# Attention values by Strassen's seven products for the eight longest pairs of query tiles

## The chip, the cores and the metric

The kernel runs on one core of one Trainium2 chip. A core has a matrix engine (PE, with its weight loads shown apart as PEld), a vector engine (DVE), a scalar engine (ACT), a general engine (POOL), and a queue that here only issues transfers (SP). Each engine works through its own list of instructions in order; engines wait for each other by semaphores. The metric is the device time of one execution in microseconds (us), as the median of several runs.

## The reference

A layer norm of x (2 sequences of 2048 tokens, 512 wide) feeds a causal attention and, beside it, a mixture of eight experts; the result is x + attention * silu(experts). Everything is FP32. Cut to what the change touches:

```python
scores = jnp.einsum('bsk,btk->bst', q, k) * scale
scores = jnp.where(causal[None], scores, -jnp.inf)
attn = jax.nn.softmax(scores, axis=-1)
out = attn @ v
...
x = x + s * g
```

## The kernel before

The program has three stages. The first normalises x, projects queries (with the key projection folded in) and values (with the output projection folded in), and routes tokens to experts. The second runs the experts. The third, from about 632 us on, is the attention; the change is in it alone.

The order of all instructions is written out by hand (`tc.manual_schedule()`): each engine's list is what the Python code emits for it, in that order. Tiles come from pools with a fixed number of buffers; a tile that needs a buffer still in use makes its first writer wait.

**Attention by steps.** A query tile is 128 rows; there are 16 tiles per sequence, 32 in all, taken in the order of `seq`. A key block is 512 keys (`kp2`, `vp` hold such blocks of keys and values). A query tile whose causal range is n times 128 keys is said here to have length n. The main loop (the last `for s` of the kernel) does in step s:

1. `fetch_inputs` of a tile, which loads its rows of x; `attended(s-3)`: ACT scales the finished values out of PSUM (L978), DVE adds the normed x (L981); `emit(s-4)`: POOL multiplies by the gate and adds x (L989, L990), and SP stores.
2. `chunk_scores(s, j)`: for each key block, four matmuls into one PSUM bank of pool `ps_a` (L836), then DVE masks (L841) and takes the row maximum (L842). Between these, `join_p(s-1, j)`: DVE puts the two 16-bit halves of the transposed probabilities of step s-1 together again (L922).
3. `divisor(s-1)`, then `end_scores(s)`: the maximum over the blocks (L854).
4. `exponentials(s)`: ACT takes exp of each block (L907), POOL splits it into two 16-bit halves (L911), SP issues a transposing transfer for each (L916).
5. `fetch_parts`: SP issues loads of coming key, value and query blocks. In odd steps also `gather_y` (POOL gathers expert outputs, L957) and `gate` (DVE, L968 and L969, two tiles at once; ACT, Silu, L973).
6. `values(s-2)`: n matmuls of 512 columns into one PSUM bank of pool `ps_b` (L933).

So the matrix engine's list is scores(s), values(s-2), scores(s+1), values(s-1), and so on; between the scores of a tile and its values lie the values of step s-2, the scores of s+1, the values of s-1 and the scores of s+2. The last two tiles (`AHEAD`) have their gate made early (`make_ahead`), so that after the last matmul only two DVE operations and a store are left (`emit_ahead`, L1010 and L1011).

The first sequence is taken from its longest tile to its shortest (lengths 16, 15, ..., 1). The second goes, in lengths, 9, 10, 1, 2, 11, 12, 3, 4, 5, 6, 7, 8, 13, 14, 15, 16.

Of the kernel before, what the change touches and what calls it, by code (L numbers as in the profile page):

```python
# [10 lines left out]
F32 = mybir.dt.float32  # L11
BF16 = mybir.dt.bfloat16
I32 = mybir.dt.int32
U16 = mybir.dt.uint16
# [12 lines left out]
def gated_attention_moe(  # L27
# [650 lines left out]

    assert B == 2 and NBB == 4
    seq = [t for t in reversed(range(NBB * BT))]  # L680
    seq += [NBB * BT + t for t in (8, 9, 0, 1, 10, 11, 2, 3, 4, 5, 6, 7, 12, 13, 14, 15)]
    assert all(seq[s] // 2 == seq[s + 1] // 2 for s in range(0, NT, 2))
    fetch_k = fetch(aks, lambda: kp2, kt_d, "k2", "kT")
    fetch_v = fetch(avs, lambda: vp, v_d, "v2", "v")
    NQ = 4
    early = [(fetch_k, b, c) for b in range(NBB) for c in range(ND)]
    early += [(fetch_q, n, c) for n in range(NQ) for c in range(2)]

# [171 lines left out]
    stage_a.close()  # L860
    kp2 = right(att, name="kp2", bufs=NBB)
    qp2 = right(att, name="qp2", bufs=NQ)
    ps_b = psum(att, name="ps_b", bufs=2)
    ps_a = psum(att, name="ps_a", bufs=6)
    sm = right(att, name="sm2", bufs=4)


# [23 lines left out]
    wp.close()  # L891

    left = lambda **k: att.enter_context(tc.tile_pool(reuse_waits="tile", **k))
    pp = left(name="pp", bufs=4)
    php = left(name="php", bufs=4)
    tp = left(name="tp", bufs=2 * NBB)
    vp = left(name="vp2", bufs=NBB + 1)
    op = left(name="op", bufs=4)

    def exponentials(s):  # L900

        _, nm, chunks = scored.pop(s)
        rs = sm.tile([P, NBB], F32, name=f"rs_{s}", tag="rs")
        sums[s], halves[s], turned[s] = rs, [], []
        for j, w in enumerate(widths[s]):
            pr = pp.tile([P, TB], F32, name=f"pr_{s}_{j}", tag="pr")
            nc.scalar.activation(  # L907
                pr[:, :w], chunks[j][:, :w], AF.Exp, bias=nm, accum_out=rs[:, j : j + 1]
            )
            pu = php.tile([P, 2 * TB], U16, name=f"pu_{s}_{j}", tag="pu")  # L910
            nc.gpsimd.tensor_copy(  # L911
                pu[:, : 2 * w].rearrange("p (h d) -> p h d", h=2),
                pr[:, :w].bitcast(U16).rearrange("p (d h) -> p h d", h=2),
            )
            puT = php.tile([P, 2 * BT, P], U16, name=f"puT_{s}_{j}", tag="puT", bufs=6)
            nc.sync.dma_start_transpose(out=puT[:, : 2 * w // P, :], in_=pu[:, : 2 * w])  # L916
            halves[s].append(puT)

    def join_p(s, j):
        w = widths[s][j]  # L920
        pT = tp.tile([P, TB], F32, name=f"pT_{s}_{j}", tag="pT")
        nc.vector.tensor_copy(  # L922
            pT[:, :w].bitcast(U16).rearrange("p (i t h) -> p i t h", t=P, h=2),
            halves[s][j][:, : 2 * w // P, :].rearrange("p (h i) t -> p i t h", h=2),
        )
        turned[s].append(pT)

    def values(s):
        first = place(s)[2]
        po = ps_b.tile([P, D], F32, name=f"po_{s}", tag="b")  # L930
        pairs = [(j, i) for j, w in enumerate(widths[s]) for i in range(w // P)]
        for k, (j, i) in enumerate(pairs):
            nc.tensor.matmul(  # L933
                po, lhsT=turned[s][j][:, ts(i, P)], rhs=avs[first + j][:, i, :],
                start=(k == 0), stop=(k == len(pairs) - 1),
            )
        outs[s] = po

    def divisor(s):
        ri = sm.tile([P, 1], F32, name=f"ri_{s}", tag="ri")  # L940
# [3 lines left out]

    def fetch_inputs(s):
        n = seq[s]
        xt = op.tile([P, D], F32, name=f"xo_{s}", tag="xo", bufs=6)
        nc.sync.dma_start(out=xt, in_=xb[:, n, :])
        gates[s] = [xt]

# [11 lines left out]

    def gate(s):

        g = op.tile([P, 2, D], F32, name=f"g_{s}", tag="g", bufs=4)
        for i in range(2):
            w = [share[k][:, 0, seq[s + i] : seq[s + i] + 1] for k in range(2)]
            nc.vector.tensor_scalar(g[:, i, :], rows.pop((s + i, 0)), w[0], None, ALU.mult)  # L968
# [4 lines left out]
        nc.scalar.activation(g, g, AF.Silu)  # L973

    def attended(s):
        o = op.tile([P, D], F32, name=f"o_{s}", tag="o", bufs=3)
        n = seq[s]
        nc.scalar.activation(  # L978
            o, outs[s], AF.Identity, scale=sums[s], bias=xshift[:, n : n + 1]
        )  # L980
        nc.vector.scalar_tensor_tensor(  # L981
            o, gates[s][0], xscale[:, n : n + 1], o, ALU.mult, ALU.add
        )
        outs[s] = o
# [12 lines left out]
    def make_ahead(s):  # L997
        xt, g = gates[s]
        n = seq[s]
        w = op.tile([P, D], F32, name=f"w_{s}", tag="w", bufs=2)  # L1000
        nc.vector.tensor_scalar(w, g, xscale[:, n : n + 1], 1.0, ALU.mult, ALU.add)
        nc.vector.tensor_tensor(xt, xt, w, ALU.mult)
        nc.vector.scalar_tensor_tensor(
            xt, g, xshift[:, n : n + 1], xt, ALU.mult, ALU.add
        )

    def emit_ahead(s):
        xt, g = gates.pop(s)
        o = op.tile([P, D], F32, name=f"o_{s}", tag="o", bufs=3)
        nc.vector.scalar_tensor_tensor(o, outs.pop(s), sums[s], g, ALU.mult, ALU.mult)  # L1010
        nc.vector.tensor_tensor(o, o, xt, ALU.add)  # L1011
        nc.sync.dma_start(out=ob[:, seq[s], :], in_=o)

    K = NBB
    parts_b = [(0, fetch_v, 0), (1, fetch_v, 1), (1, fetch_v, 2), (2, fetch_v, 3),
               (3, fetch_v, K + 2), (4, fetch_k, K + 2), (7, fetch_v, K + 1), (8, fetch_k, K + 1),
               (11, fetch_v, K), (12, fetch_k, K), (15, fetch_v, K + 3), (16, fetch_k, K + 3)]
    parts_b = [(s, f, b, c) for s, f, b in parts_b for c in range(ND)]  # L1020
    parts_b += [(2 * n - 5, fetch_q, n, c) for n in range(NQ, NT // 2) for c in range(2)]
    parts_b.sort(key=lambda part: part[0])

    def fetch_parts(s, most):
        while parts_b and most and parts_b[0][0] <= s:
# [2 lines left out]
            most -= 1  # L1028

    for s in range(NT + OUT + 2):  # L1030
        if s < NT and s:
            begin_scores(s)
        if s < 3:
            fetch_parts(s, 2 * ND)
        for k in range(NT):
            if s == (NT - 5 if k in AHEAD else k + 1):
                fetch_inputs(k)
        if 0 <= s - 3 < NT:
            (emit_ahead if s - 3 in AHEAD else attended)(s - 3)
        if 0 <= s - OUT < NT and s - OUT not in AHEAD:  # L1040
            emit(s - OUT)
        late = s - 1 if 0 <= s - 1 < NT else None
        joins = list(range(len(widths[late]))) if late is not None else []
        if s < NT:
            for j in range(len(widths[s])):
                if s:
# [2 lines left out]
                    join_p(late, joins.pop(0))  # L1049
        for j in joins:  # L1050
            join_p(late, j)
        if 0 <= s - 1 < NT:
            divisor(s - 1)
        if s < NT:
# [3 lines left out]
            fetch_parts(s, 4)  # L1058

        for k in range(0, NT, 2):  # L1060
            if s == (k - 1 if k in AHEAD else k + 3):
                gate(k)
        for k in range(0, NT, 2):
            if s == (k - 3 if k in AHEAD else k + 1):
                gather_y(k)
                gather_y(k + 1)
        for k in AHEAD:
            if s == min(k, NT - 2):
                make_ahead(k)
        if 0 <= s - 2 < NT:  # L1070
            values(s - 2)
    att.close()

# [43 lines left out]
```

## Time and profile before

| What | Value |
| --- | --- |
| median of 3 runs | 1095.23 us (1094.83 to 1099.15) |
| the profiled execution, time | 1094.91 us |
| the profiled execution, span of its trace | 1093.2 us |
| granted PE clock, mean | 0.999 of full speed |
| PE busy | 1079.4 us, 99% of the span |
| DVE, ACT, POOL busy | 484.5, 323.5, 392.8 us |
| attention scores, PE (L836) | 239.1 us, 640 records |
| attention values, PE (L933) | 238.5 us, 544 records |
| PE idle before L933 | 2.1 us |

An FP32 matmul leaves two records of its weight load and two of its multiplication, so 544 records are 272 matmuls. The number after "x" in a row counts records. "Busy" of a group is the time that at least one of its instructions ran; since matmuls overlap, it is less than the count times the mean duration. "Idle before" is time in which that engine stood still just before these instructions, with what ended it.

### The profile page before, as it was taken

How to read it: one execution, taken by the hardware profiler on the slowest of the kernel's cores; microseconds unless marked ns; L12 is line 12 of the kernel's file. 1: busy time of each engine (PE TensorE's matmuls, PEld its weight loads, DVE VectorE, ACT ScalarE, POOL GpSimd, SP SyncE). 2: the span in 40 equal slices, each digit the busy share in tenths (PEclk: the TensorE clock that was granted, in tenths of full speed). 3: DMA queues.
4: the chain of work that ended last, by engine and by line, in shares of the span. 5: the costliest groups of instructions: out<-in, count | busy, mean ns of one | idle time of the engine just before them, and what ended most of it. 6: DMA issues, size and time to landing. Idle time of an engine off the chain costs nothing.

```text
span 1093.2 us, 10842 instructions
## 1 busy us (share of the span) xinstructions
PE 1079.4 (99%) x3044; PEld 521.2 (48%) x3044; DVE 484.5 (44%) x982; ACT 323.5 (30%) x680; POOL 392.8 (36%) x443
## 2 busy tenths in 40 slices
PE   8999999999999999999999999999999999999998
PEld 3444444444555555555545444444454444444443
DVE  4535441686333333333345342333445565464542
ACT  3232323211333232323256121321323333333220
POOL 2411120002443333333331031443546677575530
PEclk9999999999999999999999999999999999999999
DMA  8989889925999999999985185454567886474520
GB/s 306 245 250 289 251 225 339 299 106 143 185 252 229 224 232 226 230 221 233 219 190 148 34 231 127 128 129 123 157 185 195 254 243 166 142 209 113 128 49 29
DMA packets 306218, 210.03 MB, mean 192 GB/s; under 512 B 238056, under 2 KB 250344, under 8 KB 305136
## 3 DMA queue, kind: packets, MB, share of 16 engines
q1 hardware_dynamic: 284080, 146.91, 54.3%
q0 software_dynamic: 10560, 35.17, 12.4%
q10 hardware_dynamic: 11520, 27.27, 6.7%
q8 instruction: 26, 0.43, 0.2%
q14 instruction: 32, 0.26, 0.1%
HBM read 92.89 MB, written 60.03 MB: 140 GB/s over the span
## 4 chain that ended last, share of the span: by engine, by line
PE 74%; issue 12%; POOL 7%; DMA 3%; ACT 2%; DVE 1%; SPq 1%; ACTq 0%; POOLq 0%; DVEq 0%
PE ph L752 15%; PE py L791 15%; PE ps L836 11%; PE po L933 10%; PE pj L324 10%; PE pj L329 9%; PE pw L200 3%; POOL pu L911 2%; POOL yg L957 2%; DMA puT<-pu 2%; POOL o L990 1%; POOL o L989 1%; PE pg L290 1%; ACT w1c L733 1%; POOL xs L638 1%
## 5 line engine op out<-in xcount | busy, mean ns | idle before, releaser
L933 PE MATMUL po<-v,pT 128*128 128x512 f32 x544 | 238.5, 592 | 2.1 <-DVE ri L941 1.7
L836 PE MATMUL ps<-k,q 128*128 128x512 f32 (+3 forms) x640 | 239.1, 529 | 0.0
L791 PE MATMUL py<-w,ht 128*128 (+3 forms) x408 | 187.1, 593 | 0.0
L836 PEld LDWEIGHTS ps<-k,q 128*128 128x128 f32 x640 | 117.7, 190 | 126.7 <-issue 118.3
L752 PE MATMUL ph<-w,xT 128*128 (+1 forms) x544 | 173.1, 460 | 0.7 <-POOL keep L874 0.7
L933 PEld LDWEIGHTS po<-v,pT 128*128 128x128 f32 x544 | 102.7, 190 | 123.9 <-issue 119.8
L911 POOL COPY pu<-pr 128x1024 uint16<-128x1024 uint16 (+3 forms) x80 | 79.7, 1028 | 209.4 <-ACT pr L907 196.9
L777 ACT ACTIVATE ht<-ht,b1sel 128x128 f32<-128x128 f32 (+3 forms) x237 | 73.1, 375 | 230.7 <-DVE ht L771 230.7
L752 PEld LDWEIGHTS ph<-w,xT 128*128 128x128 f32 (+1 forms) x544 | 97.4, 181 | 73.2 <-issue 34.3
L762 POOL COPY hu<-h 128x704 uint16<-128x704 uint16 x68 | 52.6, 773 | 206.7 <-ACT h L760 155.0
L799 DVE COPY y<-py 128x512 f32<-128x512 f32 x68 | 46.9, 690 | 172.7 <-PE py L791 169.0
L324 PE MATMUL pj<-kT,wqk 128*128 128x512 f32 x256 | 113.2, 595 | 0.0
L329 PE MATMUL pj<-wvo,kT 128*128 128x512 f32 x256 | 113.0, 594 | 0.0
L791 PEld LDWEIGHTS py<-w,ht 128*128 128x128 f32 (+3 forms) x408 | 73.5, 182 | 75.5 <-issue 38.1
L638 POOL DMA_INDIRECT xs<-zu_d,toki x68 | 68.9, 1014 | 69.3 <-DVE toki L538 57.9
L907 ACT ACTIVATE pr<-ps,nm 128x512 f32<-128x512 f32 (+3 forms) x80 | 49.0, 620 | 139.1 <-DVE nm L854 138.9
L981 DVE SCALAR_TENSOR_TENSOR o<-xo,xscale,o 128x512 f32<-128x512 f32 x30 | 28.6, 953 | 133.3 <-ACT o L978 118.6
L334 ACT COPY j<-pj 128x512 f32<-128x512 f32 x64 | 37.4, 584 | 142.8 <-PE pj L329 65.6
L842 DVE TENSOR_REDUCE mx<-ps 128x1 f32<-128x512 f32 (+3 forms) x80 | 48.8, 610 | 65.4 <-PE ps L836 64.3
L247 POOL COPY zu<-z 128x1024 uint16<-128x1024 uint16 x32 | 36.1, 1128 | 115.1 <-DVE z L232 115.1
L324 PEld LDWEIGHTS pj<-kT,wqk 128*128 128x128 f32 x256 | 47.6, 190 | 59.2 <-issue 55.0
L329 PEld LDWEIGHTS pj<-wvo,kT 128*128 128x128 f32 x256 | 47.7, 190 | 58.0 <-issue 55.5
(160 smaller groups left out, 896.6 us busy)
## 6 DMA issues: line engine op xcount, KB each, us to landing
y_d<-y SPq DMA_DIRECT2D x68, 256.0 KB
zu_d<-zu SPq DMA_DIRECT2D x32, 264.0 KB
x<-in_x_dram SPq DMA_DIRECT2D x32, 256.0 KB
kt_d<-kT ACTq DMA_DIRECT2D x8, 1024.0 KB
qt_d<-j ACTq DMA_DIRECT2D x32, 256.0 KB
v_d<-j ACTq DMA_DIRECT2D x32, 256.0 KB
k<-kt_d SPq DMA_DIRECT2D x32, 256.0 KB
q<-qt_d SPq DMA_DIRECT2D x32, 256.0 KB
```

Source lines behind the costliest of these rows:

```text
L324: nc.tensor.matmul(po, lhsT=wqk[:, c, ts(r, P)], rhs=kT[:, c, :], start=(c == 0), stop=(c == ND - 1),)
L329: nc.tensor.matmul(po, lhsT=kT[:, c, ts(r, P)], rhs=wvo[:, c, :], start=(c == 0), stop=(c == ND - 1),)
L638: nc.gpsimd.indirect_dma_start(out=xs, out_offset=None, in_=zu_d, in_offset=bass.IndirectOffsetOnAxis(ap=toki[:, i : i + 1], axis=0),)
L752: nc.tensor.matmul(ph[at, :], lhsT=xT[:, c, at], rhs=rhs[k], start=(c == 0), stop=(c == ND - 1),)
L762: nc.gpsimd.tensor_copy(hu[:, :, :H], h.bitcast(U16).rearrange("p (d h) -> p h d", h=2))
L777: nc.scalar.activation(ht[:hn, c, at], ht[:hn, c, at], AF.Silu, bias=b1sel[:hn, c, j : j + 1])
L791: nc.tensor.matmul(py[at, :], lhsT=ht[:k, c, at], rhs=rhs[n], start=(c == 0), stop=(c == NH - 1),)
L836: nc.tensor.matmul(ps[:, :w], lhsT=aqs[seq[s] // 2][:, c, ts(t % 2, P)], rhs=aks[first + j][:, c, :w], start=(c == 0), stop=(c == ND - 1),)
L842: nc.vector.tensor_reduce(scored[s][0][:, j : j + 1], ps[:, :w], AX.X, ALU.max)
L907: nc.scalar.activation(pr[:, :w], chunks[j][:, :w], AF.Exp, bias=nm, accum_out=rs[:, j : j + 1])
L911: nc.gpsimd.tensor_copy(pu[:, : 2 * w].rearrange("p (h d) -> p h d", h=2), pr[:, :w].bitcast(U16).rearrange("p (d h) -> p h d", h=2),)
L933: nc.tensor.matmul(po, lhsT=turned[s][j][:, ts(i, P)], rhs=avs[first + j][:, i, :], start=(k == 0), stop=(k == len(pairs) - 1),)
```

## The change

Two query tiles and two blocks of 128 keys form a 2x2 block product, as do the two halves of the 512 value columns: A (probabilities, two tiles by two key tiles) times B (two key tiles by two column halves). Done plainly that is eight products of 256 columns (the kernel before does them as four of 512). The change does it with seven, by Strassen's scheme in Winograd's form, for the pairs listed in `FAST`: the four longest pairs of the first sequence and the four longest of the second. A pair of lengths (n1, n2) has m = min(n1, n2) // 2 such blocks; with lengths (15,16), (13,14), (11,12) and (9,10), m is 7, 6, 5 and 4, so 22 per sequence and 44 in all. Key tiles beyond 2m (three per pair) are multiplied plainly, in halves of 256 columns (`product`).

What is added around the products:

- `combine_v(b)`: four DVE operations on each value block; for sequence 1 in steps 1 and 2, between the joins and `end_scores`; for sequence 2 in steps 21, 22, 23 and 25.
- `combine_p(s)`: four DVE operations on m times 128 columns each. In the even step after a pair's scores, all joins and `combine_p` are put ahead of that step's score maxima.
- `values_first` and `values_begin` (even step), `values_end` (odd step) in place of `values`: seven chains of m matmuls, two chains to a PSUM bank (left and right half), with two ACT copies and eight DVE additions of 256 columns between them.
- For the pair of the last two steps but two, `values_begin` is moved one step later; the last pair's gate (`gate`, `make_ahead`) is made in step 32 and not before step 31.

What is moved or resized: the second sequence goes in lengths 7, 8, 1, 2, 5, 6, 3, 4, 9, 10, ..., 16; `parts_b` loads value blocks 0 and 1 before the first transposes and 2 and 3 in step 1; buffers are cut (`pp` 4 to 3, `pu` 4 to 3, `puT` 6 to 5, gathered rows 4 to 2, gates 4 to 2, `xo` 6 to 5, `ps_a` 6 to 5, queries 4 to 3, values 5 to 4 blocks), `ps_b` has 3 banks in place of 2, and `attended` and `emit` of a fast pair come at its fourth and fifth step.

```diff
-    seq += [NBB * BT + t for t in (8, 9, 0, 1, 10, 11, 2, 3, 4, 5, 6, 7, 12, 13, 14, 15)]
+    seq += [NBB * BT + t for t in (6, 7, 0, 1, 4, 5, 2, 3, 8, 9, 10, 11, 12, 13, 14, 15)]
-    ps_b = psum(att, name="ps_b", bufs=2)
-    ps_a = psum(att, name="ps_a", bufs=6)
+    ps_b = psum(att, name="ps_b", bufs=3)
+    ps_a = psum(att, name="ps_a", bufs=5)
...
+    FAST = (0, 1, 2, 3, 12, 13, 14, 15)
...
+    def combine_v(b):
+        n = 1 if b % NBB == NBB - 1 else 2
+        v = avs[b].rearrange("p (i h) d -> p i h d", h=2)[:, :n]
...
+        nc.vector.tensor_tensor(t1, b12, b11, ALU.subtract)
+        nc.vector.tensor_tensor(t2, b22, t1, ALU.subtract)
+        nc.vector.tensor_tensor(t3, b22, b12, ALU.subtract)
+        nc.vector.tensor_tensor(t4, b21, t2, ALU.subtract)
...
+    def combine_p(s):
+        m = min(place_keys(s), place_keys(s + 1)) // 2
...
+        nc.vector.tensor_tensor(s1, a21, a22, ALU.add)
+        nc.vector.tensor_tensor(a21, a11, a21, ALU.subtract)
+        nc.vector.tensor_tensor(s2, s1, a11, ALU.subtract)
+        nc.vector.tensor_tensor(s4, a12, s2, ALU.subtract)
...
+    def chain(dst, a, v, stop=True):
+        n = a.shape[1]
+        for k in range(n):
+            nc.tensor.matmul(
+                dst, lhsT=a[:, k], rhs=v(k), start=(k == 0), stop=(stop and k == n - 1)
+            )
...
+    def values_first(s):
+        p16, u2 = bank(s, "p16"), half_d(s, "u2")
+        chain(p16[:, LO], combos[s][1], raw(s, 0, LO))
+        nc.scalar.copy(u2, p16[:, LO])
+        seven[s] = p16, u2
+
+    def values_begin(s):
...
+        chain(p75[:, LO], s3, vt(s, 2))
+        chain(p16[:, HI], s2, vt(s, 1))
+        nc.scalar.copy(o1[:, LO], u2)
+        add(u2, p16[:, HI], u2)
+        add(u3, p75[:, LO], u2)
...
+    def values_end(s):
...
+        chain(p75[:, HI], s1, vt(s, 0))
+        add(o2[:, HI], p75[:, HI], u3)
+        add(u2, p75[:, HI], u2)
+        p24 = bank(s, "p24")
+        chain(p24[:, LO], a12, raw(s, 1, LO), stop=False)
+        product(p24[:, LO], s, 2 * m, k1, LO, start=False)
+        add(o1[:, LO], p24[:, LO], o1[:, LO])
+        chain(p24[:, HI], a22, vt(s, 3), stop=False)
+        product(p24[:, HI], s + 1, 2 * m, k2, LO, start=False)
+        add(o2[:, LO], p24[:, HI], u3)
+        p03 = bank(s, "p03")
+        product(p03[:, LO], s + 1, 2 * m, k2, HI)
+        add(o2[:, HI], p03[:, LO], o2[:, HI])
+        if s + 1 in AHEAD:
+            emit_ahead(s + 1, o2, slice(0, D))
+            emit_ahead(s, o1, LO)
+        chain(p03[:, HI], s4, raw(s, 1, HI), stop=False)
+        product(p03[:, HI], s, 2 * m, k1, HI, start=False)
+        add(o1[:, HI], p03[:, HI], u2)
...
-    parts_b = [(0, fetch_v, 0), (1, fetch_v, 1), (1, fetch_v, 2), (2, fetch_v, 3),
-               (3, fetch_v, K + 2), (4, fetch_k, K + 2), (7, fetch_v, K + 1), (8, fetch_k, K + 1),
-               (11, fetch_v, K), (12, fetch_k, K), (15, fetch_v, K + 3), (16, fetch_k, K + 3)]
+    parts_b = [(0, fetch_v, 0), (0, fetch_v, 1), (1, fetch_v, 2), (1, fetch_v, 3),
+               (4, fetch_k, K), (6, fetch_v, K), (8, fetch_k, K + 1), (10, fetch_v, K + 1),
+               (12, fetch_k, K + 2), (14, fetch_v, K + 2), (16, fetch_k, K + 3), (18, fetch_v, K + 3)]
...
+    combine = {1: [0, 1], 2: [2, 3], 21: [K], 22: [K + 1], 23: [K + 2], 25: [K + 3]}
...
+        fast = s // 2 - 1 in FAST
...
+        if fast and s % 2 == 0:
+            for j in joins:
+                join_p(late, j)
+            joins = []
+            combine_p(s - 2)
...
+        for b in combine.get(s, []):
+            combine_v(b)
...
-            if s == (k - 1 if k in AHEAD else k + 3):
+            if s == (k + 2 if k in AHEAD else k + 3):
                 gate(k)
...
+        if s == NT:
             for k in AHEAD:
                 make_ahead(k)
-        if 0 <= s - 2 < NT:
+        if fast:
+            if s == NT - 1:
+                values_begin(s - 3)
+            if s % 2:
+                values_end(s - 3)
+            else:
+                values_first(s - 2)
+                if s != NT - 2:
+                    values_begin(s - 2)
+        elif 0 <= s - 2 < NT:
             values(s - 2)
```

## The prediction

> **What bounds the kernel now.** First the page's busy times, then the PE rows with each tile shape apart.
>
> ```profile
> PE 1079.4 (99%) x3044; PEld 521.2 (48%) x3044; DVE 484.5 (44%) x982; ACT 323.5 (30%) x680; POOL 392.8 (36%) x443
> ```
>
> ```profile
> L933 PE MATMUL po<-v,pT 128*128 128x512 f32 x544 | 238.5, 592 | 2.1 <-DVE ri L941 1.7 <-DVE pT L922 0.3
> L836 PE MATMUL ps<-k,q 128*128 128x512 f32 x448 | 196.7, 593 | 0.0
> L836 PE MATMUL ps<-k,q 128*128 128x256 f32 x64 | 15.1, 379 | 0.0
> ```
>
> PE is never waiting: the values stand still for 2.1 us in all, the scores for none. So PE work removed is time gained, but every wait put before PE is time lost, one for one. 593 less 379 says that 256 columns cost about 214 ns per record in a stream; weight loads of one stream start every 0.43 us at 512 columns. So a 512-column FP32 matmul (two records) takes 0.86 us, a 256-column one 0.43 us, with no extra price for the narrower form (its busy time over its count, 236 ns, still holds the ends of 8 short runs and is the upper bound).
>
> Next the timeline around the last scores (step 31), for what DVE, ACT and POOL take. Columns: start us, duration us, engine, line, [idle before].
>
> ```profile
> 1050.02 0.30 DVE L841 TENSOR_TENSOR ps<-ps,keep 128x128 f32<-128x128 f32 x1 [2.14 <-PE ps L836]
> 1051.69 0.14 DVE L854 TENSOR_REDUCE nm<-mx 128x1 f32<-128x4 f32 x1
> 1054.22 1.41 DVE L969 SCALAR_TENSOR_TENSOR g<-yg,share,g 128x512 f32<-128x512 f32 x1
> 1062.04 0.78 ACT L978 ACTIVATE o<-po,xshift,ri 128x512 f32<-128x512 f32 x1 [4.96 <-PE po L933]
> 1062.90 0.75 DVE L981 SCALAR_TENSOR_TENSOR o<-xo,xscale,o 128x512 f32<-128x512 f32 x1 [7.27 <-ACT o L978]
> 1063.57 4.63 DVE L922 COPY pT<-puT 128x1024 uint16<-128x1024 uint16 x4
> 1063.73 1.65 POOL L989 TENSOR_TENSOR o<-o,g 128x512 f32<-128x512 f32 x1 [3.66 <-DVE o L981]
> 1075.75 0.69 DVE L1011 TENSOR_TENSOR o<-o,xo 128x512 f32<-128x512 f32 x1
> ```
>
> The row maximum (nm) is there 1.8 us after the scores end (1049.98), the gate 3.8 us after nm. Four joins take 4.63 us beside POOL's emits; alone they take 0.61 each. A DVE tensor-tensor is 0.29 at 128 columns and 0.69 at 512: estimate 0.43 at 256, 0.69 at 512, 1.09 at 896. Last the one real PE wait, to see what a hand-over costs: the join ended at 848.83, and PE started 0.15 later.
>
> ```profile
> 848.02 0.82 DVE L922 COPY pT<-puT 128x768 uint16<-128x768 uint16 x1 [1.58 <-DMA puT<-pu]
> 848.98 0.67 PE L933 MATMUL po<-v,pT 128*128 128x512 f32 x1 [1.74 <-DVE ri L941]
> ```
>
> [...] The change puts two chains in one bank, and its program does wait there; no run yet shows the price. [...]
>
> **The change part by part.**
>
> *PE work removed.* Per block, four 512-column matmuls (8 x 0.429 = 3.43 us) become seven of 256 (14 x 0.215 = 3.01): 0.41. Times 44: **-18.0** (-9 if a record costs 236 ns against 438.5 for 238.5/544). The 24 leftover key tiles cost the same in halves.
>
> *Added DVE and ACT work* costs nothing as work (DVE is 44% busy): four operations per value block, four per pair of up to 1.09 us, eight adds of 0.43, two small ACT copies. It costs where it stands in line ahead of what PE waits for. I followed the order of each engine's list in the changed program, with the durations above.
>
> *B, bank hand-over.* In `values_end` the right half of p24 waits for the DVE add that reads the left half, and likewise p03. Nothing else is in PE's list between. Price: PE drain 0.16 (379 less 216), DVE start 0.04, add 0.43, restart 0.15, and the second record after a restart comes 0.08 late: 0.85. For p03, six pairs (the last two are under Tail): **+5.1**.
>
> *A, the same for p24, with DVE busy.* In DVE's order the adds stand behind nm and `gate` of that odd step. The add is done at scores' end + 1.3 to 1.9 (nm, read from the timeline in steps 3, 5, 7, 9, 21, 29) + 3.8 (gate) + 0.7 (two adds) + 0.43 + 0.15 = 6.4 to 6.9 us. PE gets there after two chains and one or two leftover tiles, 0.43 each: 6.9, 6.0, 5.2, 4.3 us (m = 7, 6, 5, 4, first sequence), 3.9 and 4.8 (m = 4, 5, second). Stalls 0.85, 1.0, 1.6, 2.5, 3.1, 1.7: **+10.7**.
>
> *C, the s2 chain.* It goes into the bank whose left half ACT copies (u2), and that copy is behind the exponentials of the same step. Scores' end to last exp is 5.6, 4.8, 4.9, 4.5, 4.7 us in steps 4, 6, 8, 20, 28 of before; with 0.55 for copy and restart, less what joins no longer delay, and 1 us more in step 8 where `combine_p` comes ahead of the maxima. PE has two chains, 2m x 0.43 = 5.2, 4.3, 3.5, 3.5, 4.3. Stalls **+6.7** (0.4, 1.0, 2.5, 1.5, 0.9, restarts 0.4).
>
> *Start.* Before: joins of step 0 end 646.9, nm(1) 647.3, scores(2) end 657.4, last join of step 1 659.8, nm(2) 660.1. Now block 1's loads are ahead of the transposes on SP (+1, some of it hidden), then `combine_v` of blocks 0 and 1 (8 x 0.69 = 5.5) precedes nm(1): 653.8. With five score banks, the second block of scores(2) waits for the first exp of tile 1: 654.6 for 648.8, so scores(2) end at 663.2. Joins of step 1 end 12.6 after nm(1) as before: 666.4. `combine_p` 4.4: 670.8. Maxima 2.5: 673.3. `combine_v` of 2 and 3, 4.5: 677.8; nm(2) 678.2; exps 2.6; u2 and restart 0.6: 681.4; s2 chain of 3.0: 684.4. Without stalls the three chains would end at 657.4 + 9.1 = 666.5. **+18**.
>
> *Tail.* Step 31: u3 is behind the gate, s1's chain waits for it, 1.5; A and B for the last two pairs, 4 x 0.85 = 3.4. Step 32: T is the end of `values_end(28)`. DVE first finishes two tiles (add, ACT 0.78, L981 twice: T + 3.0), and only then joins tile 31 and combines. POOL's four emit operations fall on this: joins 2.5 alone, 4.6 beside two, about 6 beside four; then two combinations: s3 at T + 10.4, while PE has one chain (3.0). Stall 7.5. Then s2 and s4, gate 2.5, Silu 1.1, `make_ahead` 3.6, u2, u3 are ahead of s1's chain: 11.2 us, while PE has two chains (6.0): 5.2. **+17.6**. After the last matmul three half-width operations and a half store take the place of two and a store: nothing.
>
> *Middle.* Where tiles are short, the time from the scores' end to the first join is 11 to 12 us (steps 13, 16, 17 of before, where PE did stall). The cover before values(16), (17), (20), (21) is 12, 11, 12, 14 lengths x 0.86 = 10.3, 9.4, 10.3, 12.0, and step 21 has a `combine_v` (2.7) ahead of nm. POOL's smaller buffers and SP's moved loads fall here: the new key and value blocks are issued behind that step's transposes, 1.9 us each, and need free blocks that PE has left a step before. +6 less the stalls of before: **+4** (0 to 10).
>
> Sum: -18 + 5.1 + 10.7 + 6.7 + 18 + 17.6 + 4 = +44. The profiled span 1093.2 becomes 1137; the execution's time is 1.7 above its span and the median 0.3 above that: **1139 us**.
>
> **The rivals.** (1) Only the bank hand-overs cost (A and B at 0.85, 16 times = 13.6), as start and tail find cover: 18 - 13.6 gives 1091, the same; with half of C, A and Tail, 1101 to 1118. For it: ACT and DVE are under half busy. Against: the waits are of order, not of load. (2) **The other side:** the seven products show. The place is `values_end`; if a hand-over costs 0.3 in place of 0.85 and DVE's queue has drained by then, 18 less about 8 gives 1085. It decides where all waits together fall below 18; Start or Tail alone reach that, so it is unlikely. (3) The short tiles become the bound: POOL needs about 6.7 us per step there (4 gathers per two steps, two emits, a copy) against 6.6 of PE, so a backlog delays copies, transposes and values: 20 more, 1152 to 1170. (4) 256-column matmuls are not half: the gain is 9, 1148; it lies within the range. For it only the 236 ns.
>
> **Numbers.** A measurement tells 0.5% (5.5 us) from no change. All waits as listed 0.70 (1119 to 1151, (4) in it); partly covered 0.09; short tiles bound 0.10; same 0.06; faster 0.05. Slower is 0.89. The range 1108 to 1156 takes in the first case, half of the second and half of the third. Its ends also follow from the terms' own: start 10 to 21, tail 12 to 21, middle 0 to 10, gain 9 to 18.
>
> **What would show it.** Right: 256-column records 0.215 us apart in the values; PE idle of some 60 us before the values' lines, put down to the DVE adds, ACT's u2 copy and the combinations; about 18 of it between 645 and 685 and as much in the last 60; gaps of 0.8 us or more in each `values_end`. Wrong: a start without a PE gap (then the V combinations were faster, or nm(1) was not behind them); `values_end` without gaps; or PE idle mostly in the short tiles.

## The result and the profile after

The change makes the kernel slower: 1169.99 us median of 4 runs (1167.6 to 1170.79) against 1095.03 (1094.27 to 1099.15) for the kernel before, a ratio of 1.0673 (95% interval 1.0641 to 1.0704). That is 75 us more, where +44 was predicted; it lies above the range. The profiled span grew by 72.7 us, from 1093.2 to 1165.9.

The page of the changed kernel, busy times first, then the granted PE clock in 40 slices of the span:

```profile
PE 1089.1 (93%) x3356; PEld 588.3 (50%) x3356; DVE 552.4 (47%) x1112; ACT 328.9 (28%) x696; POOL 392.9 (34%) x443
...
PEclk9999999999999999999999889999999999899989
```

PE has less to do and yet is busy for longer (1089.1 for 1079.4): some of its records ran at half pace, which the 8s of the clock line show (the mean granted clock is 0.977, before 0.999). Waits are read from one execution of each kernel; its time stands beside the median in the table of the experiments, since the two are up to 6 us apart. The rows of PE from 630 us on, tile shapes apart (busy, mean ns, idle before and its releasers):

```profile
L836 PE MATMUL ps<-k,q 128*128 128x512 f32 x416 | 185.8, 600 | 7.4 <-ACT pr L908 7.4
L942 PE MATMUL po<-v,pT 128*128 128x512 f32 x144 | 68.0, 619 | 10.5 <-DVE pT L924 8.8 <-DVE ri L1055 1.7
L989 PE MATMUL p<-vT,pT 128*128 128x256 f32 x176 | 49.2, 433 | 25.9 <-DVE pT L981 13.9 <-DVE o L1006 9.9 <-DVE vT L964 2.1
L989 PE MATMUL p<-vT,s 128*128 128x256 f32 x176 | 44.6, 405 | 13.5 <-ACT u L1011 9.0 <-DVE u L1006 4.5
L989 PE MATMUL p<-v,s 128*128 128x256 f32 x88 | 21.1, 388 | 4.1 <-DVE o L1006 4.1
```

Before, these columns held 2.1 us of idle in all; now 65.4 (with the 4.0 us of shorter scores). The releasers are the ones named in the prediction: L981 is the combination that the s3 chain needs, L1006 the adds that free a bank (A and B), L1011 the copy of u2 (C), L908 the exponentials that free a bank of scores. The chains of a pair follow each other on PE as a11, s3, s2 (`values_begin`) and s1, a12, a22, s4 (`values_end`), named by the operand made of probabilities; A is the wait before a22, B that before s4, C that before s2. The L942 row, ordinary values of short tiles, now waits 10.5 us, 8.8 of it for joins. In PE's timeline (start, duration, what, idle before and releaser):

```profile
656.38 11.69 PE L836 MATMUL ps<-k,q 128*128 128x512 f32 x24 [7.41 <-ACT pr L908]
...
679.58 4.75 PE L989 MATMUL p<-vT,s 128*128 128x256 f32 x14 [2.36 <-ACT u L1011]
...
702.95 3.29 PE L989 MATMUL p<-vT,pT 128*128 128x256 f32 x14 [0.52 <-DVE o L1006]
...
989.56 3.60 PE L989 MATMUL p<-vT,pT 128*128 128x256 f32 x8 [5.16 <-DVE pT L981]
996.84 3.55 PE L989 MATMUL p<-vT,s 128*128 128x256 f32 x8 [3.69 <-ACT u L1011]
...
1017.38 3.52 PE L989 MATMUL p<-vT,pT 128*128 128x256 f32 x8 [2.81 <-DVE o L1006]
...
1134.24 6.10 PE L989 MATMUL p<-vT,pT 128*128 128x256 f32 x14 [8.76 <-DVE pT L981]
```

Start, hand-overs, copy of u2 and tail are all there. Two things are not in the prediction: the wait at 989 with most of that at 997, and the durations behind long waits. 14 records of 256 columns take 3.29 us at 702.95 and 6.10 at 1134.24. The 24 records at 656.38 (16 of 512 columns and 8 of 256, merged in one line) take 11.69, where the same 24 take 8.86 in runs shown below: here the ones of 512 columns stand 0.854 us apart for a while, and 0.429 after it.

By stages, from the records of the trace: idle is the gap to the end of the record before, and drain the 0.1 to 0.2 us that this last record takes beyond its usual distance to a next one; slow is the distance between records above 0.429 us x columns/512 where there was no gap.

| Stage (us of the span) | Predicted | Idle and drain | Slow records | Before, both |
| --- | --- | --- | --- | --- |
| 630 to 685, start | 18.0 | 12.7 | 4.0 | 0.0 |
| 685 to 830, first long pairs | 13.7 | 10.8 | 3.0 | 0.2 |
| 830 to 985, short tiles | 4.0 | 15.4 | 5.4 | 2.8 |
| 985 to 1085, second long pairs | 8.9 | 16.3 | 5.4 | 0.1 |
| from 1085, tail | 17.6 | 16.6 | 3.9 | 0.0 |

The columns of after sum to 71.8 and 21.7; less before's 3.1 and less 18 of work that is 72.4, and the spans grew by 72.7. So about 29 us are missing in the prediction: 14 in the short tiles, 13 in the second long pairs, 3 in the tail, less 1 too much at the start. In the short tiles 5.8 us belong to one place: at 966 the third block of scores(25) waits 4.04 us for a bank that the exponentials of step 24 free, and DVE's combinations of V in steps 22 and 23 (5.1 and 2.5 us) stand ahead of nm in that line.

### The profile page after: what moved, and what is told of

Read it like the earlier page. It is cut to its first block, busy times and chain, and to the rows that moved or that the text cites. A ratio compares the mean times of both kernels' runs of the same rounds, so it can differ in the third digit from the quotient of the medians.

```text
span 1165.9 us, 11696 instructions
## 1 busy us (share of the span) xinstructions
PE 1089.1 (93%) x3356; PEld 588.3 (50%) x3356; DVE 552.4 (47%) x1112; ACT 328.9 (28%) x696; POOL 392.9 (34%) x443
## 5 line engine op out<-in xcount | busy, mean ns | idle before, releaser
L836 PE MATMUL ps<-k,q 128*128 128x512 f32 (+3 forms) x640 | 243.9, 537 | 11.5 <-ACT pr L908 11.5
L836 PEld LDWEIGHTS ps<-k,q 128*128 128x128 f32 x640 | 119.6, 194 | 135.5 <-issue 112.0
L908 ACT ACTIVATE pr<-ps,nm 128x512 f32<-128x512 f32 (+3 forms) x80 | 49.1, 621 | 180.8 <-DVE nm L854 180.6
L942 PE MATMUL po<-v,pT 128*128 128x512 f32 x144 | 68.0, 619 | 10.5 <-DVE pT L924 8.8
L989 PE MATMUL p<-vT,pT 128*128 128x256 f32 x176 | 49.2, 433 | 25.9 <-DVE pT L981 13.9
L924 DVE COPY pT<-puT 128x1024 uint16<-128x1024 uint16 (+3 forms) x80 | 58.5, 749 | 31.1 <-DMA puT<-pu 31.1
```

The lines of the kernel that those rows point to most:

```text
L836: nc.tensor.matmul(ps[:, :w], lhsT=aqs[seq[s] // 2][:, c, ts(t % 2, P)], rhs=aks[first + j][:, c, :w], start=(c == 0), stop=(c == ND - 1),)
L908: nc.scalar.activation(pr[:, :w], chunks[j][:, :w], AF.Exp, bias=nm, accum_out=rs[:, j : j + 1])
L924: nc.vector.tensor_copy(turned[s][:, j * TB : j * TB + w].bitcast(U16).rearrange("p (i t h) -> p i t h", t=P, h=2), halves[s][j][:, : 2 * ...
L942: nc.tensor.matmul(dst, lhsT=turned[s][:, ts(k, P)], rhs=avs[first + k // BT][:, k % BT, cols], start=(start and k == k0), stop=(k == k1 - 1),
L989: nc.tensor.matmul(dst, lhsT=a[:, k], rhs=v(k), start=(k == 0), stop=(stop and k == n - 1))
```

## The experiments

The theory at the outset: the waits of the scheme as predicted, and PE's half pace behind them, for the rest. The rivals: the short tiles in their new order are the bound by themselves; the half pace has another cause than idleness; the waits only move when one is removed.

| Run | Median us | Profiled run, us | Ratio to before (95%) |
| --- | --- | --- | --- |
| the change | 1169.99 | 1167.60 | 1.0673 (1.0641 to 1.0704) |
| frame: no products | 1110.64 | 1115.04 | 1.0133 (1.0117 to 1.0150) |
| trim: six pairs | 1139.77 | 1145.45 | 1.0403 (1.0386 to 1.0420) |
| warm: stalls filled | 1172.98 | 1173.72 | 1.0704 (1.0679 to 1.0730) |
| banks: halves in turns | 1156.44 | 1155.68 | 1.0559 (1.0534 to 1.0583) |
| frame_order | 1102.37 | 1100.15 | 1.0052 (1.0034 to 1.0071) |
| frame_banks | 1106.90 | 1104.86 | 1.0102 (1.0073 to 1.0130) |
| u2early | 1161.24 | 1156.74 | 1.0598 (1.0567 to 1.0628) |
| gate_late | 1180.15 | 1179.36 | 1.0771 (1.0749 to 1.0794) |
| best1: six pairs, old order | 1125.61 | 1125.33 | 1.0269 (1.0242 to 1.0296) |
| best2: four pairs, old order | 1090.70 | 1092.19 | 0.9948 (0.9933 to 0.9964) |
| best3: five pairs, old order | 1089.41 | 1088.12 | 0.9944 (0.9927 to 0.9961) |
| plain2: best2 without products | 1099.04 | 1095.92 | 1.0026 (1.0018 to 1.0033) |

### Without the products: what the frame costs

```diff
-    FAST = (0, 1, 2, 3, 12, 13, 14, 15)
+    FAST = ()
```

(`combine_v` is left out; `gate`, `make_ahead` and `emit_ahead` of the last pair go back to their old steps and form, and with them the buffers of `xo` and of the gates to 6 and 4.)

> Every pair gets its values by the ordinary product; the second batch's order, the smaller buffers, the 5+3 PSUM banks and the loads' times are those of the changed kernel. If the loss is the waits of the scheme and the slow clock behind them, the frame alone costs 4 to 8 us over the kernel before: 1099 to 1103. If the short tiles together, the order or the missing buffers bound the middle (rival 3), its 20.7 us of idle and slow records stay although no combination is computed: 1112 to 1120.

Measured 1110.64: 15 us over the kernel before, not 4 to 8, and just under the rival's numbers. PE's timeline of this run:

```profile
651.03 11.91 PE L836 MATMUL ps<-k,q 128*128 128x512 f32 x24 [2.83 <-ACT pr L908]
...
855.87 5.46 PE L942 MATMUL po<-v,pT 128*128 128x512 f32 x6 [3.06 <-DVE ri L1055]
...
880.18 6.25 PE L942 MATMUL po<-v,pT 128*128 128x512 f32 x14 [2.10 <-DVE pT L924]
...
916.16 6.23 PE L942 MATMUL po<-v,pT 128*128 128x512 f32 x10 [3.54 <-DVE pT L924]
```

and its busy times from 830 to 985 (length of the window, then PE, PEld, DVE, ACT, POOL with their counts, clock, DMA share, GB/s):

```profile
830.00:985.00 155.00, 143.82 (x371) 69.13 (x370) 84.91 (x167) 56.66 (x96) 101.58 (x91) 0.97 0.73 204
```

The short tiles lose 17.4 us (12.0 idle and drain, 5.4 slow) with no combination in the program; with the products they lose 20.8. The two sums are not made of the same waits: the frame, which combines no V, has none before scores, so the 5.8 us at 966 are the products' own. And the frame's profiled run is its slowest, 1115.04 us at a mean granted clock of 0.991; the other three took 1109.79 to 1111.11 at 0.995 to 0.997, so some 4 us of slow records and waits are not in the usual run. After 985 the frame has no gap at all, so the 21.7 us there do belong to the products. POOL is busy 101.6 of 155 us: it is not full, so a lack of its throughput is not what holds PE. In each of the six stretches of 15 us from 850 to 940 it was busy for 9.9 to 12.1. What PE waits for is one tile's way from its scores to its last join, 13 to 20 us in steps 14 to 22 (from the ends of the L836 and L924 records).

### Order and banks apart

```diff
-    seq += [NBB * BT + t for t in (6, 7, 0, 1, 4, 5, 2, 3, 8, 9, 10, 11, 12, 13, 14, 15)]
+    seq += [NBB * BT + t for t in (8, 9, 0, 1, 10, 11, 2, 3, 4, 5, 6, 7, 12, 13, 14, 15)]
```

on the frame for frame_order (its loads of keys and values in the order that this wants), and for frame_banks, on the frame too:

```diff
-    ps_b = psum(att, name="ps_b", bufs=3)
-    ps_a = psum(att, name="ps_a", bufs=5)
+    ps_b = psum(att, name="ps_b", bufs=2)
+    ps_a = psum(att, name="ps_a", bufs=6)
```

> The frame run (ordinary products, 5+3 banks, the changed kernel's small buffers) with the second batch in the old order (8, 9, 0, 1, 10, 11, 2 to 7, 12 to 15) and the loads of its keys and values in the order in which that wants them. If the new order is what opens the 17 us of idle and slow records between 830 and 985, they go to 2 or 3 and the time to 1095 to 1099. If the five banks of scores or the smaller buffers open them, the time stays at 1108 to 1112.

> The frame run with 6 PSUM banks for scores and 2 for values, as in the kernel before; the new order stays. If the order is the cause: 1106 to 1111, only the 2.8 us wait at the start goes. If the sixth bank is: 1095 to 1099.

By the ratios the frame's 1.3% falls to 0.5% with the old order and to 1.0% with the sixth bank: the order is worth some 9 us. The bank's 3 us are not set apart from none (the two intervals overlap), but in the trace of frame_banks the wait at the start is gone with its slow records. In frame_order the stage from 830 to 985 has 5.9 us of idle and slow records left. In the old order long tiles stand between the short ones, so the same 13 to 18 us from scores to joins (steps 14 to 19 of that run) lie behind more PE work. The order is the main cause in the middle, though not to the whole extent expected (1095 to 1099; before itself stood at 1098.3 in that session).

PE's timeline of frame_order, for the start and for the wait that answers to the frame's at 855.87:

```profile
650.67 8.86 PE L836 MATMUL ps<-k,q 128*128 128x512 f32 x24 [2.18 <-ACT pr L908]
...
852.47 4.22 PE L942 MATMUL po<-v,pT 128*128 128x512 f32 x6 [3.07 <-DVE ri L1055]
```

The two kernels have the same PE list up to there. The wait at the start differs by 0.65 us (2.83 and 2.18), the 24 records behind it by 3.05 (11.91 and 8.86), and PE comes to the later wait at 852.81 and 849.40, 3.4 us apart. So what half pace costs at the start was still there 200 us on. This part of the difference between the two spans is no merit of the order.

### The ends

```diff
-    FAST = (0, 1, 2, 3, 12, 13, 14, 15)
+    FAST = (1, 2, 3, 12, 13, 14)
-    combine = {1: [0, 1], 2: [2, 3], 21: [K], 22: [K + 1], 23: [K + 2], 25: [K + 3]}
+    combine = {2: [0, 1], 3: [2], 21: [K], 22: [K + 1], 23: [K + 2]}
```

(The last pair goes out in its old form, and `values_begin` is always in the even step.)

> The first and the last pair go back to the ordinary product, six pairs keep the seven products; V is combined in steps 2 and 3. If start and tail cost what the trace of the changed kernel shows (16.7 us of idle and slow records before 685, about 17 of the 20.5 after 1085), and the two pairs give back 14/44 of the 18 us saved (5.7): 1170 - 15 - 17 + 5.7 = 1144 (1139 to 1150). If the stall of the start only moves to the next pair, and that of the tail to the pair before: 1160 or more.

Measured 1139.77, in the theory's range. Two pairs fewer give back 5.7 us of removed work and still the time falls by 30: start and tail together cost about 36 us of the change by the medians, 32 by the waits and slow records of the two traces. How much of that V's combinations ahead of nm(1) and nm(2) cost is not told apart. What is left at the ends is 3.1 us before 685 and 2.2 after 1085.

### A, B and C

For banks, the adds' order follows the chains':

```diff
-        p24 = bank(s, "p24")
+        p24, p03 = bank(s, "p24"), bank(s, "p03")
         chain(p24[:, LO], a12, raw(s, 1, LO), stop=False)
...
+        product(p03[:, LO], s + 1, 2 * m, k2, HI)
+        add(o2[:, HI], p03[:, LO], o2[:, HI])
         chain(p24[:, HI], a22, vt(s, 3), stop=False)
```

For u2early, ahead of `chunk_scores` in the main loop, and no more behind it:

```diff
+        if fast and s % 2 == 0:
+            values_first(s - 2)
```

For gate_late, the loop that calls `gate` is moved behind `values_end` (the last pair's gate stays ahead of `make_ahead`).

> The halves of p24 and p03 take turns (p24 low, p03 low, p24 high, p03 high), so no chain follows at once in the bank of the chain before. If the hand-over waits A and B are what the prediction said, some 16.6 us of gaps go (A 9.8, B 4.1, four of the tail 2.7) and a little of the slow clock: 1152 to 1157. If A's part behind the maxima and the gate only moves one chain on, B's share goes alone: 1164 to 1167.

> The changed kernel with the a11 chain and ScalarE's copy of u2 issued before the scores of the even step (and so before its exponentials) instead of after them. If C is the queue of exponentials ahead of the copy, its gaps before the s2 chains go (2.4 at the start, 0.7, 1.5, 3.7, 0.8 = 9 us, and part of the slow clock), against an a11 chain that may now wait for its joins at the start: 1158 to 1164. If the copy only moves the wait to the u3 sum or the exponentials behind it: 1167 to 1173.

> The changed kernel, with the gate of each pair but the last emitted behind the value sums of its step instead of ahead of them, and nothing else. If the prediction's A is the sum of a bank hand-over (0.68 us) and of the gate and maxima queued ahead on VectorE, the six A gaps (0.68, 0.82, 1.45, 2.33, 2.98, 1.58 us) fall to 0.68 each, 5.8 us together, and the wait for u3 in step 31 (3.42) loses 1 to 2: 1161 to 1164. If the maxima of the scores, not the gate, are what the sums stand behind, the gaps keep most of their length: 1168 or more.

banks came to 1156.44 and u2early to 1161.24, both in the theory's range, though neither gained all that the theory listed. The PE rows of banks that held A and B:

```profile
L989 PE MATMUL p<-vT,pT 128*128 128x256 f32 x176 | 48.5, 430 | 21.2 <-DVE pT L981 13.7 <-DVE o L1006 5.3 <-DVE vT L964 2.2
...
L989 PE MATMUL p<-v,s 128*128 128x256 f32 x88 | 20.3, 379 | 0.0
```

B is gone (4.1 to 0.0), A is down from 9.9 to 5.3: what remains is DVE coming late from maxima and gate, no longer the hand-over. And of u2early, where C stood, with what came new:

```profile
L989 PE MATMUL p<-vT,s 128*128 128x256 f32 x176 | 44.3, 404 | 4.7 <-DVE u L1006 4.7
L989 PE MATMUL p<-v,pT 128*128 128x256 f32 x176 | 43.2, 391 | 5.2 <-DMA v<-v_d 4.9 <-DVE pT L924 0.3
```

The 9.0 us behind L1011 are gone; 4.9 of them came back at the start, where the a11 chain, now ahead of the scores, waits for value blocks still under way.

gate_late is the miss, 10 us slower than the change. Its A gaps are all 0.52 us, as its theory said, but other waits grew, in PE's timeline:

```profile
773.69 4.63 PE L989 MATMUL p<-vT,s 128*128 128x256 f32 x10 [4.05 <-ACT u L1011]
...
1145.98 6.06 PE L989 MATMUL p<-vT,pT 128*128 128x256 f32 x14 [12.45 <-DVE pT L981]
```

They were 0.65 and 8.76. DVE's timeline of the run shows how (L1095 finishes two tiles of an earlier pair; L854 is nm of the same step):

```profile
761.39 1.46 DVE L1095 SCALAR_TENSOR_TENSOR o<-xo,xscale,o 128x512 f32<-128x512 f32 x2 [1.83 <-ACT o L1092]
...
769.97 0.14 DVE L854 TENSOR_REDUCE nm<-mx 128x1 f32<-128x3 f32 x1
```

The gate is the last thing DVE does in its step; ACT's Silu waits for it, and the finishing of tiles (ACT L1092) waits behind the Silu. DVE's next step begins with the operation that needs L1092, and behind it stand the joins, `combine_p`, the maxima and so the exponentials and the copy of u2. In the change L1095 began at 755.56 and nm was there at 764.05, 1.4 us after those scores; here at 769.97, 4.8 after. The wait had moved, and into a longer line.

### Half pace

```diff
+    IDLE = {24: 10, 30: 18}
...
+        idle_products(p75[:, LO], IDLE.get(s, 0), s)
         chain(p75[:, LO], s3, vt(s, 2))
...
+                if s == 2 and j == 1:
+                    idle_products(bank(s, "dm")[:, LO], 14, s)
```

(`idle_products` is a chain of matmuls on loaded keys and queries, whose result nobody reads.)

> Products that nobody reads fill three stalls of the changed kernel: 14 matmuls of 256 columns (6.0 us) before the second chunk of scores(2), 10 (4.3 us) before the s3 chain of pair 24, 18 (7.7 us) before that of the last pair. If TensorE falls to half speed because of the idle time, the records after these places come 0.43 us apart (512 columns) instead of 0.85 and the time falls by 6 to 10 us although work was added: 1160 to 1164. If the slow records have another cause (operands, transfers, DVE traffic), they stay, and the time is 1170 or a few us above.

PE's timeline of this run; L1017 is the filling:

```profile
648.55 6.21 PE L1017 MATMUL dm<-k,q 128*128 128x256 f32 x28
656.20 8.86 PE L836 MATMUL ps<-k,q 128*128 128x512 f32 x24 [1.45 <-ACT pr L908]
...
680.80 5.39 PE L990 MATMUL p<-vT,s 128*128 128x256 f32 x14 [2.36 <-ACT u L1012]
...
1138.80 3.29 PE L990 MATMUL p<-vT,pT 128*128 128x256 f32 x14 [1.02 <-DVE pT L982]
1144.92 4.97 PE L990 MATMUL p<-vT,s 128*128 128x256 f32 x14 [2.83 <-ACT u L1012]
```

Both halves of the expectation came out, on different sides. Half pace does come from standing still: the 24 records take 8.86 us for 11.69, the s3 chain at the end 3.29 for 6.10. But the time does not fall (1172.98; its interval overlaps that of the change). The scores of step 2 end 3 us earlier, and the s2 chain still begins at 680.80 (679.58 in the change), since V's combinations and nm on DVE come last there; at the end the faster s3 chain only waits longer for the copy of u2, which stands behind the gate's Silu. At the filled places half pace lay under a DVE or ACT line that was late anyway; in the frame (above), where PE came last, it cost its full length. So the 21.7 us of slow records are not all a loss of their own. How much of them is, no run separates.

### A version that keeps the products covered

The waits at 989 and 997 belong to the first pair behind the short tiles. A pair on seven products needs the joins of both its tiles before its second chain, while an ordinary tile needs its own alone. From the end of the second tile's scores to the place of its s3 chain PE had 14.6 us of work there (969.8 to 984.4), which is called its cover here, and the way through nm, exponentials, splitting, transposes, joins and combination took 19.8. best1 was to cover all waits at once: trim with the edits of banks and u2early, V's combinations behind the exponentials, and the old order with

```diff
+    FAST = (1, 2, 3, 8, 10, 14)
```

> Seven products for six pairs, laid so that every wait found above is covered: first and last pair ordinary, p24 and p03 in turns, u2 before the scores, V combined behind the exponentials of its step, and the old order of the second batch with pairs (8, 9), (10, 11), (12, 13) on seven products. Work removed: 18 x 30/44 = 12.3 us. If the waits were all, 1095 - 12 + 2 to 6 left over: 1085 to 1089. If a combination on VectorE still ends on the path in each pair (2 us each), 1095 or above.

Measured 1125.61: by its number that is the second case, but the waits are not of 2 us in each pair. From 985 on it has 0.7 us of idle and slow records, from 630 to 830 some 9, but the middle has 37. PE's timeline:

```profile
892.62 3.75 PE L989 MATMUL p<-vT,pT 128*128 128x256 f32 x8 [11.01 <-DVE pT L981]
...
948.39 4.60 PE L989 MATMUL p<-vT,pT 128*128 128x256 f32 x10 [10.20 <-DVE pT L981]
```

These are the pairs of lengths 9, 10 and 11, 12, behind which the old order has tiles of one and three key tiles. PE had 7.9 and 6.5 us of work from the end of the second tile's scores; the s3 chain could start 18.9 and 16.7 us after that end. So best2 takes only pairs with a long tile behind them, `FAST = (1, 2, 3, 14)`, and adds the late gate and 6+2 banks (p16 and p24 in one, p75 and p03 in the other); best3 takes the pair of lengths 7 and 8 as well, with 17.6 us of PE work; plain2 is best2 with `FAST = ()`.

> Seven products only for the four pairs that have a whole step of long scores behind their second tile: pairs 1, 2, 3 of the first batch and tiles 12, 13 of the second. Old order; 6 banks for scores and 2 for values, which the chains take in turns (a11 and s2, then p24, in one; p75, then p03, in the other); u2 before the scores; the gate's products on VectorE behind the value sums; V combined behind the exponentials. Work removed 18 x 21/44 = 8.6 us. If every wait is covered: 1095 + 2 for the frame - 8.6 + 1 = 1089 (1086 to 1092). If a wait per pair is left as before: 1097 or more.

> As best2, and tiles 6, 7 of the second batch (three block pairs) by seven products too: 1.2 us of work less. Their second tile has 5 us of ordinary values and 14 us of scores behind it. If 19 us cover its chain: 1088 (1085 to 1091). If they do not (the pairs 8, 9 and 10, 11 had about 5 us of cover in best1 and waited 10 to 11 us): a wait of 1 to 3 us and 1090 or more.

> The same kernel as best2 with no pair on seven products (no combination is computed): the frame alone. 1095 to 1098. best2 less this run is what the seven products are worth when covered: -8.6 if all of the removed work shows, 0 if the frame or a wait takes it.

best2 is at 1090.70 and best3 at 1089.41, both faster than the kernel before by half a per cent (their intervals end at 0.9964 and 0.9961; the slowest run of either, 1092.24, lies below the fastest of the kernel before in that session, 1094.43), and so than the change. The two are not told apart from each other; in best3's trace the added pair waits 0.10 us. Against plain2, its own frame, best2 gains 8.3 us of medians for 8.6 of removed work (plain2 itself lies 1 us above its expected range): what the products save shows nearly whole once almost nothing waits for them. (The profiled spans are only 3.7 us apart, 1090.5 and 1094.2, for best2's profiled run is its slowest and plain2's its fastest; the first has 4.0 us more of waits and slow records, among them one wait of 3.74 us in the short tiles, where plain2 has 1.70.) PE's rows of best2:

```profile
L942 PE MATMUL po<-v,pT 128*128 128x512 f32 x352 | 157.5, 600 | 3.7 <-DVE ri L1054 3.7
L989 PE MATMUL p<-vT,pT 128*128 128x256 f32 x84 | 19.9, 384 | 0.7 <-DVE pT L981 0.4
L989 PE MATMUL p<-vT,s 128*128 128x256 f32 x84 | 19.4, 379 | 0.0
L989 PE MATMUL p<-v,s 128*128 128x256 f32 x42 | 9.7, 379 | 0.0
```

The gate behind the sums, which lost 10 us alone, does no harm here: all of the products' rows together wait 0.7 us. The copy of u2 no longer stands behind the exponentials, and the first, last and uncovered pairs are not on products. These edits came together; their shares in this kernel were not measured.

## Why the prediction was right and wrong

The side was right: slower, at a stated chance of 0.89. The size was not, +75 for +44. By its steps:

- **PE work removed, -18.0:** right. Records of 256 columns stand 0.215 to 0.216 us apart, and best2 against plain2 shows 8.3 of 8.6 us. Rival 4 is out.
- **B, 0.85 each:** 0.52 of idle and 0.16 of drain, 0.68; six make 4.1 for 5.1. What ends the wait is the DVE add that reads the other half of the bank (0.52 <-DVE o L1006), and banks took it away by leaving a chain between (the row p<-v,s has 4.1 us of idle in the change, 0.0 in banks).
- **A, 10.7:** right, place by place: 0.68, 0.82, 1.45, 2.33, 2.98 and 1.58, 9.8 together, for 0.85, 1.0, 1.6, 2.5, 3.1, 1.7.
- **C, 6.7:** the sum is right by chance: idle of 0.65, 1.53, 3.69, 0.81, also 6.7, none in step 4, and 3.69 in step 26 for 1.5. u2early, in which these waits are gone, confirms the cause.
- **Start, +18:** 16.7 with its slow records. nm(1) at 655.5 for 653.8, the s2 chain at 679.6 for 681.4. scores(2) ended at 668.1 for 663.2, 2.8 us of it by half pace.
- **Tail, +17.6:** 20.5. u3's wait was 3.26 for 1.5 and the s3 wait 8.76 for 7.5 (the prediction's own parts, 3.0, about 6 and two combinations of 1.09, make T + 11.2 and a stall of 8.2; T + 10.4 was written). The last s1 chain waited only 1.2 for 5.2, in part since s3 had run at half pace: in warm, with s3 at full pace, s2 and s1 wait 2.83 and 1.05. 3.9 of slow records were not in the prediction. The start of that stretch is in DVE's timeline of the change:

```profile
1123.81 1.46 DVE L1095 SCALAR_TENSOR_TENSOR o<-xo,xscale,o 128x512 f32<-128x512 f32 x2 [0.88 <-ACT o L1092]
1125.18 6.76 DVE L924 COPY pT<-puT 128x1024 uint16<-128x1024 uint16 x4
1131.97 1.09 DVE L980 TENSOR_TENSOR s<-pT 128x896 f32<-128x896 f32 x1
1133.10 1.09 DVE L981 TENSOR_TENSOR pT<-pT,pT 128x896 f32<-128x896 f32 x1
```

  Four joins beside four emits of POOL (L1103 and L1104, from 1124.64 to 1131.39) take 6.76 us (predicted about 6). With POOL idle one join took 0.61 up to DVE's next operation (649.38 to 649.99 in the same trace), which makes 4 x 0.61 for four.
- **Middle, +4 (0 to 10): the step that failed.** Measured 18.0 over before, 13.0 of it idle and drain. The prediction had the place: it named values(16), (17), (20) and (21), and the first and the last two of these wait 4.04, 3.16 and 1.58. What it had wrong is the time that the cover, counted in matmuls, was set against: 11 to 12 us to the first join, read in steps 13, 16 and 17 of before. In the new order it is 13 to 20 us to the last join (frame), and before already had 20.1 and 17.3 in its own steps 18 and 19 (lengths 1 and 2). V's combinations it put at 2.7 us in step 21 and at nothing in steps 22 and 23, which end in the 5.8 us at 966. The frame loses 17.4 in this stage without a single product, and frame_order puts most of that on the order; a share of the sixth bank is not shown. Rival 3 had the place and nearly the size (+20), but not the mechanism: POOL was busy 66% of that stretch, and what was short is cover for one tile's chain.
- **The step that was missing: the pair behind the short tiles.** 5.16 us before s3 at 989 and 3.69 before s2 at 997 (the latter counted under C already), with 3.1 of slow records. The prediction took the second long pairs for the first ones again, and did not ask how much PE work lies behind the second tile of each pair. best1, with 11.0 and 10.2 us at two pairs of still less cover, shows that this is what decides.
- **Half pace behind idle time** was not thought of; the profile of before, at a mean granted clock of 0.999, gave little cause to. 21.7 us of the records are slow; part is under waits that were there anyway.

Rivals 1 and 2 are out: the waits were of order, not of load, and start and tail found no cover.

## What to carry to other kernels

Fewer matmuls are a gain only where what feeds them has cover: count, for each place, the PE work between the moment an operand's chain starts and the moment it is needed, and compare it with the chain's length (here 17 to 21 us from a tile's scores to its combined operands; the pairs with 6.5 to 15.8 us of cover waited 3.7 to 11 us for s3, those with 17.6 us or more, first and last pair apart, at most 0.4). The length is that of the line as it stands: in the tail of the change the way took 35 us, since DVE finished other tiles first, and a cover of 26 was not enough. A scheme that ties two tiles together takes a whole step of that cover away, so use it only on the pairs that can spare it: four such pairs gained 8 us over their frame, eight pairs with theirs lost 75. When a wait stands behind an engine's line, moving the work that stands ahead in that line moves the wait to whoever needs that work next; look for him before.

## What the runs showed of the hardware

In these runs half pace came mostly behind waits of about 2 us and more. Over the attention stage of all kernels here (waits of more than 0.6 us, 144 of them): below 1.9 us, 2 of 61 were followed by slow records, both soon after a longer wait; from 1.9 to 2.8, 12 of 23; from 2.8 to 3.9, 29 of 36; above, 23 of 24.

In these traces the length of a wait alone did not tell the two apart, but where it fell. In the trace of the change the 21 changes of the granted clock stand at whole multiples of 3.413 us from each other, as they do in every other trace here with several changes. Cut into stretches of that length, the attention stages of the fourteen traces show (by the modelled ends of PE's records): of the stretches at full clock in which PE stood still for 2.05 us or more, all 62 were followed by a stretch at half clock; between 1.80 and 2.05, 2 of 15; below 1.80, none of 1869. At half clock, the next stretch was at half again in all 35 cases with more than 0.7 us of standing still, and at full in all 50 with less than 0.5. In the change alone the nine with 2.15 us or more were followed by 0.50, of the three with 1.81, 1.84 and 1.97 the first, and none of the other 127 (up to 1.42 us); at half clock five with 1.10 us or more stayed there, and ten with 0.47 or less went back to 1.00. Two waits of 3.26 us show the difference, the one before 1107.68 in the change and the one before 1109.34 in warm (stretch and its length, then PE, PEld, DVE, ACT, POOL busy, granted clock, DMA share, GB/s):

```profile
1105.84:1109.25 3.41, 1.57 (x7) 1.42 (x8) 0.85 (x2) 0.86 (x2) 2.23 (x4) 1.00 0.92 176
...
1104.94:1108.35 3.41, 1.14 (x6) 0.66 (x4) 1.64 (x2) 3.38 (x7) 2.67 (x3) 1.00 0.67 129
```

In the change the wait is split over two stretches, 1.42 and 1.84 us of it, the clock stays at 1.00, and the 12 records behind it take 2.86 us. In warm 2.27 us of it fall in one stretch, the next two are granted 0.50, and the same 12 records take 5.49. The waits at the start of frame (2.17 us of it in one stretch, then 11.91 us for 24 records) and of frame_order (2.01 in one, then 8.86) differ in the same way.

What slow records cost in the change: behind the wait of 2.81 us before 1017.38, with one stretch at 0.50, 8 records of 256 columns took 3.52 us for 1.99 at 1023.14; behind the 8.76 us before 1134.24, with three at 0.50, the first of them and part of the second without work, 14 took 6.10 for 3.29 at 1152.10. By an estimate from these clocks and lengths, a stretch at 0.50 loses up to 1.7 us, half of 3.413, so that here the cost goes with the stretches at 0.50 in which PE has work and not with the length of the wait.
